# A two-layer transformer block on one core: first score maxima two tiles a block step, expert results two a step, closing projections in six pipelined steps

## The chip, the cores and the metric

The kernel runs on one core of one Trainium2 chip. The metric is the device time of one execution in microseconds, as the median of several runs. The engines are called as the profile calls them: PE (TensorE), DVE (VectorE), ACT (ScalarE), POOL (GpSimd) and SP (SyncE, which here only issues DMAs).

## The reference

Two transformer layers on x of B = 2 sequences, S = 1024 tokens and D = 128 channels, all float32:

```python
x = x + L0_attn(layernorm(x))   # 8 heads; q, k from low-rank latents, 128 + 32 wide; full softmax
x = x + L0_ffn(layernorm(x))    # shared FFN (width 352) + top-2 of 8 routed experts, per token
x = x + L1_attn(layernorm(x))   # 16 causal heads, 8 wide, with rotary embedding
x = x + L1_ffn(layernorm(x))    # 2 of 8 experts (GELU), chosen for a sequence by its first token
```

An FFN of layer 0 is `silu(x @ gate) * (x @ up) @ down`; a routed expert's result is weighted by its normalised router probability and added to the token's row. The second FFN is the mean of its two experts' results.

## The kernel before

**Stages.** Layer 0's attention runs to about 454 us. Its last pass carries the router of batch 0 beside it. Then comes the experts stage: the routed blocks of batch 0 (23 blocks of 128 tokens sorted by expert, plus two steps to drain), the shared expert for batch 0 and for batch 1 (two groups of 512 tokens each), and the routed blocks of batch 1. After it a short tail finishes the first score maxima of layer 1. Then eight passes `i = 1..8` do layer 1's attention, one group of four heads of one sequence each (`NG` = 4 groups): pass `i` finds the row maxima of group `i` beside the attention of group `i - 1`, so pass 8 has attention alone. Last come the closing projections and the second FFN of the last sequence.

**Order.** Most of the kernel is a set of Python generators. Each `yield` ends one step. A main generator is advanced by one step, then each of its "extras" by one; the engines' queues hold the instructions in just that program order, on PE, DVE, POOL and SP (and on ACT too up to pass 3), so nothing overtakes what stands ahead of it on its engine. `hurry(g, n)` runs n steps of g in one, `spread(g, n)` one step of g in n, `after(n, g)` starts g n steps later, and `wait_for(key, g)` holds g back until the key stands in the list `passed` (this is program order, not a wait on the chip). In the experts stage one main step is one routed block, or a third of a shared group's gate and up projection, or its down projection.

**What runs beside the experts stage.**
- `route(b)` (L287): layer norm, router logits, top two, then sums along tokens (`cums`, L321 and L324, on DVE) and their matmuls `rk` (L330 to L334), from which the sorted list of rows comes. Batch 0's is hurried by two beside layer 0's last pass, batch 1's by three in `rows1` (L965).
- The gathers of rows into blocks (L456, POOL), one a step where they run.
- `combine(b, half)` (L933): eight indirect DMAs on POOL (L938), each of which fetches 128 expert results of 64 KB from DRAM (`ys`, written by L919) and adds them to one column block of x, 4 column blocks for each of the two choices. For batch 0 they run beside the shared expert, one a step. The shared expert adds its own results to the same column blocks of x with a DVE add a group (L851).
- `heads0` (L1168 on): layer norm, Q and K of batch 0 for layer 1, each split in three bf16 parts (L1044 writes these to DRAM), and `fetch(0)`, then `fetch(1)` (L1078; 18 DMAs on SP each, L1085), which bring a group's parts back in the layout for the scores. `both_heads` starts each half when that half of `combine` has passed.
- `maxima(0)`: the first group's row maxima.

**The row maxima (`maxima(i)`, L1095).** A tile is 128 rows of four heads' scores: two matmuls (L1112), a mask (L1117) and a DVE reduction (L1122). A pass has 20 tiles in two halves. After each half the maxima are split in three bf16 parts (L1160, L1162 on POOL), transposed on PE (`tp_m`, L1126), and sent by DMA as three more rows of the scores' operands. The tiles' banks come from a PSUM pool of two slots, which the block steps' gate and up projections (`gub`, L880) and the shared expert's (`gu`, L834) share.

**After the experts stage** batch 1's results are combined (`results1`), then its heads (`heads1`), beside the tail and the first passes. `attend` (L1211) makes transposed scores (L1227), the exponential on ACT (L1232), the causal mask on POOL (L1236) and the values (L1252). `finish(b, half)` (L1331) closes half a sequence: for four strips of 128 tokens, transposes (L1339), reciprocal of the sums and product (L1344, L1346), and a transpose back (L1352, copied by ACT in L1353); then the output projection (L1357), its add to x (L1361), the layer norm, the first expert matmul (L1373), GELU (L1375), the second (L1381), the result (L1386) and its DMA (L1389).

Of the kernel before, what the change touches and what calls it, by code (L numbers as in the profile page):

```python
# [13 lines left out]
F32 = mybir.dt.float32  # L14
# [35 lines left out]
def two_layers(ctx: ExitStack, tc: tile.TileContext, a: dict, out: bass.AP):  # L50
# [128 lines left out]
    def spread(steps, n):  # L179

        for _ in steps:
            for _ in range(n):
                yield
# [30 lines left out]
    def after(n, steps, every=1):  # L214
        for _ in range(n):
            yield
        yield from spread(steps, every)
# [69 lines left out]
    def route(b, bank, spare):  # L287
# [34 lines left out]
        for i in range(3):  # L322
# [1 line left out]
            nc.vector.tensor_tensor(  # L324
                cums[i + 1][:, PAD:], cums[i][:, PAD:], cums[i][:, PAD - m : PAD + NT - m], ALU.add
            )
        yield
        yield
        rk = bank()[:, 0 : (NT + 1) * NE].rearrange("p (n e) -> p n e", e=NE)
        nc.tensor.matmul(rk[:, 0:NT], tri, h0[:, PAD:], start=True, stop=False)  # L330
        nc.tensor.matmul(
# [482 lines left out]
    def bank1():  # L814
        return sa.tile([P, 512], F32, tag="sa", name="bank1")
# [117 lines left out]
    def combine(b, half):  # L933

        pos = routed[b][1]
        for k in range(2):
            for n in range(4 * half, 4 * half + 4):
                nc.gpsimd.indirect_dma_start(  # L938
                    out=x[:, b * NT + n, :], out_offset=None, in_=ys_d[b],
                    in_offset=bass.IndirectOffsetOnAxis(ap=pos[:, k, n : n + 1], axis=0),  # L940
                    bounds_check=NBLK * P - 1, oob_is_err=True, compute_op=ALU.add,
                )
                yield
# [21 lines left out]
    def rows1():  # L965

        yield from hurry(route(1, bank1, spare1), 3)
        rows = get(1)
        while "blocks" not in passed:
            next(rows, None)  # L970
            yield
        for _ in range(2):
            next(rows, None)
            yield
        for half in range(2):
            for n, _ in enumerate(combine(0, half)):
                if n % 2:
                    next(rows, None)
                yield
            passed.append(half)  # L980
        yield from rows
# [91 lines left out]
    def wait_for(what, steps):  # L1073
        while what not in passed:
            yield
        yield from steps
# [18 lines left out]
    def maxima(i):  # L1095

        qp, kp = qkp[i % 3]
        mx = small.tile([P, 4, NT], F32, name="mx")
        mx2 = small.tile([P, 4, NT // 2, 2], F32, name="mx2")
        ready = []  # L1100

        def tile_of(st, c, heads):

            s0 = st * P
            c0, c1 = 512 * c, min(s0 + P, 512 * c + 512)
            w = c1 - c0
            sc = banks()
            if len(heads) == 4:
                sc = sc.rearrange("p a (b w) -> p (a b) w", b=2)
            for n, j in enumerate(heads):  # L1110
                diag = c1 == s0 + P
                nc.tensor.matmul(  # L1112
                    sc[:, n, 0:w], qp[0:KP, j, s0 : s0 + P], kp[0:KP, j, c0:c1],
                    start=True, stop=not diag,
                )
                if diag:
                    nc.tensor.matmul(  # L1117
                        sc[:, n, w - P : w], identb, mask_st, start=False, stop=True
                    )
            hs = slice(heads[0], heads[-1] + 1)  # L1120
            to = mx[:, hs, st] if st < NT // 2 else mx2[:, hs, st - NT // 2, c]
            nc.vector.tensor_reduce(to, sc[:, :, 0:w], AX.X, ALU.max, negate=True)  # L1122

        def send(half, mp):
            tp = sa.tile([48, P], BF16, tag="sa", name="tp_m")
            nc.tensor.transpose(tp, mp.rearrange("p k j n -> p (k j n)"), identb)  # L1126
            mt = small.tile([48, P], BF16, name="mt")
            nc.vector.tensor_copy(mt, tp)
            md = tc.dram_tile([48, P], BF16, name=f"md{i}_{half}")
            nc.sync.dma_start(md, mt)  # L1130
            nc.sync.dma_start(
                qp[KP : KP + 3, :, 512 * half : 512 * (half + 1)].rearrange(
                    "k j (n s) -> k j n s", s=P
                ),
                md.rearrange("(k j n) s -> k j n s", k=3, j=4),
            )

        def take():
            if ready and ready[0][0] == 0:
                ready.pop()[1]()  # L1140
            elif ready:
                ready[0][0] -= 1

        for half in halves(i):
            for st in range(4 * half + 3, 4 * half - 1, -1):
                for c in range(half + 1):
                    w = min(st * P + P - 512 * c, 512)
                    for heads in ((0, 1, 2, 3),) if w <= 256 else ((0, 1), (2, 3)):
                        tile_of(st, c, heads)
                        take()  # L1150
                        if (st, c, heads[-1]) != (4 * half, half, 3):
                            yield
            m4 = mx[:, :, 4 * half : 4 * half + 4]
            if half:
                nc.vector.tensor_tensor(m4, mx2[:, :, :, 0], mx2[:, :, :, 1], ALU.min)
            mp = small.tile([P, 3, 4, 4], BF16, name="mp")
            rest = m4
            for k in range(3):
                if k < 2:
                    nc.gpsimd.tensor_copy(mp[:, k], rest)  # L1160
                    r = small.tile([P, 4, 4], F32, name=f"mr{k}") if k == 0 else mp[:, 2]
                    nc.gpsimd.tensor_tensor(r, rest, mp[:, k], ALU.subtract)  # L1162
                    rest = r
            ready.append([1, lambda half=half, mp=mp: send(half, mp)])
            yield
        late.append(ready.pop()[1])

    def both_heads(b, xt):  # L1168

        halves = [heads(b, half, xt) for half in range(2)]  # L1170
        ready = [2 * b + half for half in range(2)]
        return [wait_for(n, after(6 if b == 0 else 3, h)) for n, h in zip(ready, halves)]

    def heads0():
        xt = xt_pool.tile([P, S], F32, name="xt")
        for _ in hurry(zip_longest(*both_heads(0, xt)), 2):
            yield
        yield
        passed.append("fetched")
        yield from after(4, fetch(1))  # L1180

    def results1():
        for half in range(2):
            yield from spread(combine(1, half), 2)
            passed.append(2 + half)

    def heads1():
        xt = xt_pool.tile([P, S], F32, name="xt")
        for _ in zip_longest(*both_heads(1, xt)):
            yield  # L1190

    late = []
    first_maxima = wait_for("fetched", maxima(0))
    with tc.manual_schedule(engines=ALL_IN_ORDER):
        for _, kp in qkp:

# [134 lines left out]
    def finish(b, half):  # L1331


        ot = o_pool.tile([P, 512], F32, name="ot")
        for i in range(4):
            s0 = (4 * half + i) * P
            tp = bank1().rearrange("p (h d) -> p h d", d=WH)
            for gr in range(NG):
                nc.tensor.transpose(  # L1339
                    tp[:, 4 * gr : 4 * gr + 4, :], us[NG * b + gr][:, s0 : s0 + P], ident  # L1340
                )
            yield
            rden = small.tile([P, H1], F32, name="rden")
            nc.vector.reciprocal(rden, tp[:, :, DH])  # L1344
            o = o_pool.tile([P, H1 * DH], F32, name="o")
            nc.vector.tensor_tensor(  # L1346
                o.rearrange("p (h d) -> p h d", d=DH), tp[:, :, 0:DH],
                rden.unsqueeze(2).to_broadcast([P, H1, DH]), ALU.mult,
            )
            yield  # L1350
            po = bank1()
            nc.tensor.transpose(po[:, 0:P], o, ident)  # L1352
            nc.scalar.copy(ot[:, i * P : (i + 1) * P], po[:, 0:P])  # L1353
            yield
        py = bank1().rearrange("p (n d) -> p n d", d=D)
        for i in range(4):
# [39 lines left out]
    for i in range(1, n + 1):  # L1396
        passes = []
        if i < n:
            passes.append(maxima(i))
        passes.append(attend(i - 1))  # L1400
        if i + 1 < n:
            extras.append(after(1, fetch(i + 1)))
        b, gr = divmod(i, NG)
        if gr == 1:
            extras.append(after(4, choose(b), 3))
        if gr == 0:

            first, other = halves(i - 1)
            extras.append(after(18 if first else 9, finish(b - 1, first)))
            extras.append(after(30, finish(b - 1, other)))  # L1410
        with tc.manual_schedule(engines=ALL_IN_ORDER if i < 4 else IN_ORDER):
            extras = beside(zip_longest(*passes), extras)
            if i == n:
                flush()
                extras = beside((), extras, True)
# [78 lines left out]
```

## Time and profile before

| what | value |
|---|---|
| median of 3 runs | 1015.2 us (1012.77 to 1024.3) |
| the profiled execution | 1025.0 us, span 1023.2 us, mean granted PE clock 0.927 |
| PE busy | 909.4 us (89% of the span) |
| DVE, ACT, POOL busy | 587.9, 424.2, 414.9 us |
| chain that ended last | PE 66%, DVE 17%, issue, DMA and POOL 4% each |

The page lists busy time of each engine, then its busy tenths in 40 slices of 25.6 us with the clock granted to PE, then the chain that ended last and the costliest groups of instructions. A row of the timeline reads: start and length in us, engine, line, operation, output and inputs, count, and in brackets the engine's idle time before it and what ended that. The waits view adds up such idle times: line and tile that waited, what for, us in total, how often, the longest. A busy PE includes matmuls at half clock.

### The profile page before, as it was taken

How to read it: one execution, taken by the hardware profiler on the slowest of the kernel's cores; microseconds unless marked ns; L12 is line 12 of the kernel's file. 1: busy time of each engine (PE TensorE's matmuls, PEld its weight loads, DVE VectorE, ACT ScalarE, POOL GpSimd, SP SyncE). 2: the span in 40 equal slices, each digit the busy share in tenths (PEclk: the TensorE clock that was granted, in tenths of full speed). 3: DMA queues.
4: the chain of work that ended last, by engine and by line, in shares of the span. 5: the costliest groups of instructions: out<-in, count | busy, mean ns of one | idle time of the engine just before them, and what ended most of it. 6: DMA issues, size and time to landing. Idle time of an engine off the chain costs nothing.

```text
span 1023.2 us, 14408 instructions
## 1 busy us (share of the span) xinstructions
PE 909.4 (89%) x5308; PEld 438.3 (43%) x5308; DVE 587.9 (57%) x1085; ACT 424.2 (41%) x694; POOL 414.9 (41%) x532
## 2 busy tenths in 40 slices
PE   3998999999999998999798996779889999899974
PEld 2533433333333333336675575433344445444333
DVE  4496454546564657746633573746755777467322
ACT  0102334444334344454231352224646765576741
POOL 2003727373846550265047510156672234144320
PEclk9799999999999999999899997859897998789987
DMA  9000000000000000014122233332312222120000
GB/s 277 15 1 1 1 2 1 1 1 1 1 2 1 1 1 21 6 34 92 26 60 29 39 69 84 70 49 35 83 36 59 33 36 32 35 40 13 3 0 21
DMA packets 34874, 33.49 MB, mean 33 GB/s; under 512 B 5804, under 2 KB 32332, under 8 KB 33644
## 3 DMA queue, kind: packets, MB, share of 16 engines
q1 hardware_dynamic: 24978, 24.09, 10.4%
q0 software_dynamic: 6592, 5.91, 4.1%
q10 hardware_dynamic: 3235, 2.58, 1.0%
q8 instruction: 43, 0.70, 0.3%
q14 instruction: 26, 0.21, 0.1%
HBM read 24.10 MB, written 8.45 MB: 32 GB/s over the span
## 4 chain that ended last, share of the span: by engine, by line
PE 66%; DVE 17%; issue 4%; DMA 4%; POOL 4%; ACT 4%; SPq 0%; POOLq 0%; ACTq 0%; DVEq 0%
PE sc L692 10%; PE sc L624 8%; PE up L1252 7%; PE ud L723 6%; PE banks L1112 5%; PE bank L1227 4%; DVE mx2a L628 4%; PE gub L880 4%; DVE rden L750 3%; DVE mx L1122 2%; PE sc L698 2%; PE gu L834 2%; PE yblk L908 2%; ACT ex L1232 1%; PE banks L1029 1%
## 5 line engine op out<-in xcount | busy, mean ns | idle before, releaser
L1122 DVE TENSOR_REDUCE mx<-banks 128x2 f32<-128x1024 f32 (+3 forms) x160 | 174.0, 1113 | 92.0 <-PE banks L1117 72.0
L628 DVE TENSOR_REDUCE mx2a<-sc 128x2 f32<-128x1024 f32 x128 | 153.8, 1219 | 113.3 <-PE sc L624 100.7
L703 ACT ACTIVATE ex<-sc 128x1024 f32<-128x1024 f32 x128 | 131.0, 1023 | 211.9 <-PE sc L698 208.8
L1232 ACT ACTIVATE ex<-bank 128x512 f32<-128x512 f32 (+2 forms) x320 | 155.9, 559 | 125.3 <-PE bank L1227 121.8
L711 POOL TENSOR_TENSOR sum<-sum,ex 128x1024 f32<-128x1024 f32 x60 | 140.1, 2349 | 38.0 <-ACT ex L703 38.0
L624 PE MATMUL sc<-key,q 64*128 64x512 f32 x512 | 149.4, 637 | 1.2 <-DVE mx2a L628 1.1
L692 PE MATMUL sc<-q,key 64*128 64x512 f32 x512 | 141.3, 616 | 8.6 <-DVE mx2a L628 8.4
L1112 PE MATMUL banks<-kp,qp 72*128 72x512 bf16 (+3 forms) x384 | 111.4, 362 | 18.3 <-DVE mx L1122 9.9
L1227 PE MATMUL bank<-qp,kp 75*128 75x512 bf16 (+3 forms) x384 | 100.5, 347 | 4.5 <-ACT ex L1232 2.8
L1236 POOL TENSOR_SCALAR_AFFINE_SELECT ex<-ex 128x128 f32<-128x128 f32 (+1 forms) x192 | 63.9, 368 | 89.3 <-ACT ex L1232 85.0
L456 POOL DMA_INDIRECT xb<-xn,row x46 | 53.0, 1152 | 103.0 <-DVE fblk L432 42.5
L1252 PE MATMUL up<-ex,vp 128*32 128x512 f32 (+3 forms) x768 | 85.6, 540 | 3.9 <-POOL ex L1236 3.9
L938 POOL DMA_INDIRECT x<-ys,pos x32 | 49.9, 1559 | 82.7 <-DMA kp<-parts 65.8
L692 PEld LDWEIGHTS sc<-q,key 64*128 64x128 f32 x512 | 49.6, 191 | 74.7 <-issue 43.1
L624 PEld LDWEIGHTS sc<-key,q 64*128 64x128 f32 x512 | 48.1, 190 | 73.5 <-issue 49.8
L723 PE MATMUL ud<-ex,val 128*32 128x512 f32 x512 | 69.5, 615 | 0.0
L1112 PEld LDWEIGHTS <-qp 72*128 72x128 bf16 x384 | 40.1, 107 | 66.2 <-issue 51.8
L880 PE MATMUL gub<-wall,xbt 128*128 x184 | 66.2, 486 | 1.8 <-ACT xbt L867 1.3
L708 POOL TENSOR_TENSOR sum<-ex,ex 128x1024 f32<-128x1024 f32 x12 | 28.2, 2347 | 74.2 <-ACT ex L703 74.2
L886 DVE TENSOR_TENSOR hds<-slb,gub 128x352 f32<-128x352 f32 x46 | 23.8, 517 | 57.0 <-ACT slb L885 56.8
L1117 PE MATMUL banks<-mask_st,identb 128*128 128x128 bf16 x256 | 53.5, 237 | 0.0
L698 PE MATMUL sc<-mr,onesb 64*128 64x512 bf16 x256 | 51.6, 382 | 0.0
(264 smaller groups left out, 1105.4 us busy)
## 6 DMA issues: line engine op xcount, KB each, us to landing
qp<-parts SPq DMA_DIRECT2D x72, 64.0 KB
kp<-parts SPq DMA_DIRECT2D x72, 64.0 KB
parts<-qk SPq DMA_DIRECT2D x24, 128.0 KB
ys<-yb SPq DMA_DIRECT2D x10, 256.0 KB
wall<-in_ffn_gate_dram SPq DMA_DIRECT2D x1, 1584.0 KB
wall<-in_ffn_up_dram SPq DMA_DIRECT2D x1, 1584.0 KB
wall<-in_ffn_down_dram SPq DMA_DIRECT2D x2, 576.0 KB
x<-in_h_dram SPq DMA_DIRECT2D x4, 256.0 KB
```

The costliest lines, as they stand in the source:

```text
L624: nc.tensor.matmul(sc[:, j, :], qs[i][pr][r, st * P : (st + 1) * P], key2[r, 512 * c : 512 * (c + 1)], start=True, stop=True,)
L628: nc.vector.tensor_reduce(mx2[:, 2 * pr : 2 * pr + 2, st, c], sc, AX.X, ALU.max, negate=True,)
L692: nc.tensor.matmul(sc[:, j, :], key2[r, k * P : (k + 1) * P], qs[i][pr][r, cols], start=True, stop=False,)
L703: nc.scalar.activation(ex, sc, AF.Exp)
L711: adder.tensor_tensor(sums[pr], sums[pr], ex, ALU.add)
L723: nc.tensor.matmul(ud[DC * j : DC * (j + 1), :], val[:, k, :], es[j // 2][:, j % 2, :], start=(k == 0), stop=(k == NT - 1),)
L880: nc.tensor.matmul(gu[:, s, 0:FF], xbts[j // 4][:, (j % 4) * P : (j % 4 + 1) * P], flat[:, bass.ds(e0 + FF * s, FF)], start=True, stop=True,)
L1112: nc.tensor.matmul(sc[:, n, 0:w], qp[0:KP, j, s0 : s0 + P], kp[0:KP, j, c0:c1], start=True, stop=not diag,)
L1122: nc.vector.tensor_reduce(to, sc[:, :, 0:w], AX.X, ALU.max, negate=True)
L1227: nc.tensor.matmul(sc[:, j, 0:w], kp[0 : KP + 3, j0 + j, t0 : t0 + P], qp[0 : KP + 3, j0 + j, lo:hi], start=True, stop=True,)
L1232: nc.scalar.activation(ex[:, :, 0:w], sc[:, :, 0:w], AF.Exp, scale=SCALE1)
L1252: nc.tensor.matmul(up[WH * j : WH * (j + 1), lo - c0 :], vps[b][:, k, h : h + WH], es[j], start=(k == 0), stop=end,)
```

## The change

It has five parts. (1) In `route`, two more steps lie between the running sums and their matmuls. (2) Batch 0's results are combined two a step beside the shared expert, with one gather behind each two; so its heads become free earlier in program order, and their start is set by 10 and 16 steps of waiting, where it was 6 for both; the wait between the last part written and `fetch(0)` grows from one step to three. (3) The first maxima run two tiles a step, and their bf16 parts are made on DVE. (4) Batch 1's results are combined one a step in place of one in two, and two fetches get guards. (5) `finish` works its four strips off in six steps, each of which holds the transposes of one strip, the products of the one before and the transposes back of the one before that; and in the last pass its second half starts after 21 steps in place of 30.

```diff
@@ -324,8 +324,8 @@
             nc.vector.tensor_tensor(
                 cums[i + 1][:, PAD:], cums[i][:, PAD:], cums[i][:, PAD - m : PAD + NT - m], ALU.add
             )
-        yield
-        yield
+        for _ in range(4):
+            yield
         rk = bank()[:, 0 : (NT + 1) * NE].rearrange("p (n e) -> p n e", e=NE)
         nc.tensor.matmul(rk[:, 0:NT], tri, h0[:, PAD:], start=True, stop=False)
         nc.tensor.matmul(
@@ -973,9 +973,8 @@
             next(rows, None)
             yield
         for half in range(2):
-            for n, _ in enumerate(combine(0, half)):
-                if n % 2:
-                    next(rows, None)
+            for _ in hurry(combine(0, half), 2):
+                next(rows, None)
                 yield
             passed.append(half)
         yield from rows
@@ -1155,11 +1154,12 @@
                 nc.vector.tensor_tensor(m4, mx2[:, :, :, 0], mx2[:, :, :, 1], ALU.min)
             mp = small.tile([P, 3, 4, 4], BF16, name="mp")
             rest = m4
+            eng = nc.gpsimd if i else nc.vector
             for k in range(3):
                 if k < 2:
-                    nc.gpsimd.tensor_copy(mp[:, k], rest)
+                    eng.tensor_copy(mp[:, k], rest)
                     r = small.tile([P, 4, 4], F32, name=f"mr{k}") if k == 0 else mp[:, 2]
-                    nc.gpsimd.tensor_tensor(r, rest, mp[:, k], ALU.subtract)
+                    eng.tensor_tensor(r, rest, mp[:, k], ALU.subtract)
                     rest = r
             ready.append([1, lambda half=half, mp=mp: send(half, mp)])
             yield
@@ -1169,28 +1169,30 @@
 
         halves = [heads(b, half, xt) for half in range(2)]
         ready = [2 * b + half for half in range(2)]
-        return [wait_for(n, after(6 if b == 0 else 3, h)) for n, h in zip(ready, halves)]
+        return [wait_for(n, after(wait, h)) for n, h, wait in zip(ready, halves, (3, 3) if b else (10, 16))]
 
     def heads0():
         xt = xt_pool.tile([P, S], F32, name="xt")
         for _ in hurry(zip_longest(*both_heads(0, xt)), 2):
             yield
-        yield
+        for _ in range(3):
+            yield
         passed.append("fetched")
         yield from after(4, fetch(1))
 
     def results1():
         for half in range(2):
-            yield from spread(combine(1, half), 2)
+            yield from combine(1, half)
             passed.append(2 + half)
 
     def heads1():
         xt = xt_pool.tile([P, S], F32, name="xt")
         for _ in zip_longest(*both_heads(1, xt)):
             yield
+        passed.append("heads1")
 
     late = []
-    first_maxima = wait_for("fetched", maxima(0))
+    first_maxima = wait_for("fetched", hurry(maxima(0), 2))
     with tc.manual_schedule(engines=ALL_IN_ORDER):
         for _, kp in qkp:
 
@@ -1332,25 +1334,30 @@
 
 
         ot = o_pool.tile([P, 512], F32, name="ot")
-        for i in range(4):
-            s0 = (4 * half + i) * P
-            tp = bank1().rearrange("p (h d) -> p h d", d=WH)
-            for gr in range(NG):
-                nc.tensor.transpose(
-                    tp[:, 4 * gr : 4 * gr + 4, :], us[NG * b + gr][:, s0 : s0 + P], ident
-                )
-            yield
-            rden = small.tile([P, H1], F32, name="rden")
-            nc.vector.reciprocal(rden, tp[:, :, DH])
-            o = o_pool.tile([P, H1 * DH], F32, name="o")
-            nc.vector.tensor_tensor(
-                o.rearrange("p (h d) -> p h d", d=DH), tp[:, :, 0:DH],
-                rden.unsqueeze(2).to_broadcast([P, H1, DH]), ALU.mult,
-            )
-            yield
-            po = bank1()
-            nc.tensor.transpose(po[:, 0:P], o, ident)
-            nc.scalar.copy(ot[:, i * P : (i + 1) * P], po[:, 0:P])
+        tps, os = {}, {}
+        for i in range(6):
+            if i < 4:
+                s0 = (4 * half + i) * P
+                tp = bank1().rearrange("p (h d) -> p h d", d=WH)
+                for gr in range(NG):
+                    nc.tensor.transpose(
+                        tp[:, 4 * gr : 4 * gr + 4, :], us[NG * b + gr][:, s0 : s0 + P], ident
+                    )
+                tps[i] = tp
+            if 0 <= i - 1 < 4:
+                tp = tps[i - 1]
+                rden = small.tile([P, H1], F32, name="rden")
+                nc.vector.reciprocal(rden, tp[:, :, DH])
+                o = o_pool.tile([P, H1 * DH], F32, name="o")
+                nc.vector.tensor_tensor(
+                    o.rearrange("p (h d) -> p h d", d=DH), tp[:, :, 0:DH],
+                    rden.unsqueeze(2).to_broadcast([P, H1, DH]), ALU.mult,
+                )
+                os[i - 1] = o
+            if i >= 2:
+                po = bank1()
+                nc.tensor.transpose(po[:, 0:P], os[i - 2], ident)
+                nc.scalar.copy(ot[:, (i - 2) * P : (i - 1) * P], po[:, 0:P])
             yield
         py = bank1().rearrange("p (n d) -> p n d", d=D)
         for i in range(4):
@@ -1399,7 +1406,7 @@
             passes.append(maxima(i))
         passes.append(attend(i - 1))
         if i + 1 < n:
-            extras.append(after(1, fetch(i + 1)))
+            extras.append(after(1, wait_for("heads1" if i + 1 == NG else "fetched", fetch(i + 1))))
         b, gr = divmod(i, NG)
         if gr == 1:
             extras.append(after(4, choose(b), 3))
@@ -1407,7 +1414,7 @@
 
             first, other = halves(i - 1)
             extras.append(after(18 if first else 9, finish(b - 1, first)))
-            extras.append(after(30, finish(b - 1, other)))
+            extras.append(after(30 if i < n else 21, finish(b - 1, other)))
         with tc.manual_schedule(engines=ALL_IN_ORDER if i < 4 else IN_ORDER):
             extras = beside(zip_longest(*passes), extras)
             if i == n:
```

## The prediction, made before the changed kernel was run

> **What bounds the kernel now.** I read the page from the top: engine shares, then the slices, then the waits and rows of the stretches that the change touches, and last the chain that ended last.
>
> ```profile
> PE 909.4 (89%) x5308; PEld 438.3 (43%) x5308; DVE 587.9 (57%) x1085; ACT 424.2 (41%) x694; POOL 414.9 (41%) x532
> ...
> PE   3998999999999998999798996779889999899974
> POOL 2003727373846550265047510156672234144320
> PEclk9799999999999999999899997859897998789987
> ```
>
> PE is the bound nearly everywhere. A change that leaves PE's work as it is, as this one does, can earn only where PE's digit is under 9: a slice is 25.6 us, so the dips to 8 and 7 at 384 and 486 us (the two route steps), to 6 7 7 from 614 to 691 us (fetch, first tiles, pass 1) and to 7 4 at the end. PEclk falls in or just behind them, so an idle PE is paid for a second time. The profiled execution took 1025.0 us (span 1023.2), the runs' median is 1015.2. I sum against 1025.0 and scale by 1015.2/1025.0 = 0.990.
>
> **1. Route: two more steps between the running sums and their matmul.** The rows of PE around the route's two ranks:
>
> ```profile
> 405.56 0.20 PE L330 MATMUL bank<-cum,tri 128*128 128x64 bf16 x1 [3.27 <-DVE cum L321]
> 406.23 0.21 PE L331 MATMUL bank<-cum,onesq 128*128 128x64 bf16 x1 [0.47 <-DVE cum L324]
> 406.38 2.08 PE L692 MATMUL sc<-q,key 64*128 64x512 f32 x4
> ...
> 493.14 0.20 PE L330 MATMUL bank<-cum,tri 128*128 128x64 bf16 x1 [3.27 <-DVE cum L321]
> ```
>
> In both, PE stands 3.27 + 0.47 = 3.7 us for a chain on DVE. Both routes are hurried (two and three of their steps in one main step), so two more yields put the matmul one main step later: 1.2 to 2.2 us of other matmuls go in front of it. I take 1.7 a route. The second gain is the clock: the four L692 after the stall took 2.08 us, four of them elsewhere in that stretch 1.13, and the block matmuls after the second stall 2.56 instead of 1.35. The Trainium skill ("TensorE: Matmul & The Clock Gate", "Part 1: The HAM clock gate") has the clock halved after an idle window of about 3.4 us and restored after as long a busy one; a stall shortened to 2 us falls under that, and the whole cold stretch goes: by that rule 1.7 us a route (half of 3.4, an estimate), by the rows 1.0 in the first four matmuls alone and as much again behind them. Twice (1.7 + 1.6) = **-6.5**, bounds -3 and -9. What is behind the matmul (list of rows, gathers) comes one step later; its gathers had several steps of slack in the trace.
>
> **2. Batch 0's results two a step: a new wait.** These accumulating DMAs add expert results into the tiles of x that the shared expert's add (L851) also writes.
>
> ```profile
> 543.80 0.69 DVE L851 TENSOR_TENSOR x<-bank,x 128x512 f32<-128x512 f32 x1 [2.59 <-PE bank L847]
> 552.85 0.69 DVE L851 TENSOR_TENSOR x<-bank,x 128x512 f32<-128x512 f32 x1 [2.59 <-PE bank L847]
> ```
> ```profile
> 544.76 1.54 POOL L938 DMA_INDIRECT x<-ys,pos  x1 [3.18 <-DVE x L851]
> 546.60 1.54 POOL L938 DMA_INDIRECT x<-ys,pos  x1 [0.30 <-issue]
> ...
> DMA to landing us min/median/max: 3.2/3.3/4.7
> ```
>
> Counted in program order, two DMAs are now ahead of the first L851, and all of half 1's are behind the second. They land just before 543.8, so they cost nothing. After the change four are ahead of the first, and twelve ahead of the second: half 1's first four included. POOL starts one each 1.85 us (544.76 to 546.60). Say the first still starts at 538.13. With the gather between them, the fourth starts at 545.04 and lands at 545.04 + 3.3 = 548.3, so the first L851 moves from 543.8 to 548.3. The fifth waits for that add (549.35), the twelfth starts seven later at 549.35 + 7 x 1.85 = 562.3 and lands at 565.6: the second L851 moves from 552.85 to 565.6. DVE is an in-order queue: behind the waiting add stand the silu products (L839, L840) of the next group, for which PE's down-projection waits, and the banks they free. PE would stand some 8.4 us, once its slots are full, and 2.6 at the first. The shift is 10.9 at the second group's end beyond what slack takes, plus about 2.1 of half clock afterwards: **+13**, bounds +3 (if PE gets further ahead than I think) and +15.
>
> Here a rule and the rows differ. The Trainium skill ("DMA: Bandwidth & Descriptors", "Anatomy of one DMA — SWDGE (gpsimd) path") fits 2.0 us + bytes/436e3, so 64 KB would land in 2.15 us (an estimate from that page); this trace has 3.3. By the rule the term is some 2 us less; I take the row. The same page's advice ("Rules for kernel authors"), issue early and wait late, speaks against this part: DMAs are put right ahead of an add that waits for them.
>
> **3. The first tile of batch 0.** Its Q and K arrive late:
>
> ```profile
> 631.83 1.01 PE L1112 MATMUL banks<-kp,qp 72*128 72x512 bf16 x2 [7.79 <-DMA ys<-yb]
> ...
> 633.27 2.55 PE L880 MATMUL gub<-wall,xbt 128*128 x4
> ```
>
> The releaser named is long done; the last load of fetch(0) (issued 625.4, L1085) is what lands at 631.6. The fetch moves three block steps earlier (a block step alone is 2.19 us), the tile one. Without part 2 the fetch lands at 631.6 - 6.6 and the tile is due at 624.0 - 2.2, a wait of 3.2 instead of 7.8. With part 2 both move 13: first tile at 638.2, so only +6.4 is left: **-6.6**. Bounds: -2.2 (the parts' way through DRAM isn't earlier) to -9.
>
> **4. Two tiles a step, parts on DVE.**
>
> ```profile
> PE tp_m L1126 <- POOL mp L1162: 10.1, 2, 5.6
> PE banks L1112 <- DMA ys<-yb: 7.8, 1, 7.8
> ```
>
> The 10.1 us: batch 0's parts queue on POOL behind batch 1's results (L938, 1.85 each). On DVE they are four small operations (POOL took 0.20 to 0.22 for three of them, 0.7 for the first), so about 1.0 in all stays exposed. Before, 8 steps with one tile took 2.74 each and 12 lone tiles 1.23 each (DVE's maxima, 1.1 each, set that). After, a step with two tiles: gate and up 1.19, transposes and down-projection 1.0, the second tile 0.44 after its bank comes free, the maxima 1.2: about 3.9, because both use the two slots of one PSUM pool. Nine of these, 2.5 of tail and 1.0 for parts: 638.2 + 38.6 = 676.8. Before, pass 1 began at 670.8. But the last block's ys now goes out about 20 us later in relation, and fetch(1)'s last load is issued at about 674; landing as fetch(0)'s did, pass 1 begins at 679: +8.2, of which 5.6 is given back since the second wait for POOL stood inside pass 1. So +2.6 where part 3 left +6.4: **-3.8**, bounds -8 and +3.
>
> **5. Batch 1's results one a round.** They need 16 x 1.85 = 29.6 us of POOL, and now start near 678 rather than 659, beside pass 1's selects (L1236), for which the values wait. A plain round takes 1.43 us, less than one DMA: POOL sets the first 14 rounds. I take +2.0 (bounds 0 and +6). Given back: batch 1's heads are through in pass 2, so its POOL work leaves the rounds where the values waited for POOL at 760 to 764 and PE ran on a half clock to 777; I take -2.8 of that 3.7 us wait and its cold stretch. Sum **-0.8**. The guards on the fetches never bind: what they wait for ends earlier in program order.
>
> ```profile
> core 0: us, PE busy (x) PEld busy (x) DVE busy (x) ACT busy (x) POOL busy (x), PEclk, DMA share, GB/s
> 652.00:671.00 19.00, 12.01 (x60) 6.43 (x59) 13.46 (x16) 0.00 (x0) 9.74 (x10) 0.58 0.43 73
> 671.00:721.40 50.40, 41.63 (x230) 17.55 (x229) 28.78 (x46) 20.64 (x42) 29.95 (x55) 0.79 0.29 40
> 984.00:1023.20 39.20, 20.13 (x84) 13.14 (x82) 11.58 (x38) 6.62 (x13) 4.12 (x12) 0.74 0.05 14
> ```
>
> **6. The end.** 39.2 us after the last attention, PE busy 20.1. The chain there, cut to the second half's part:
>
> ```profile
> 998.81 0.69 DVE res L1386
> ...
> 1003.59 1.72 PE bank L1357 x8
> 1005.33 0.70 DVE x L1361
> ...
> 1012.66 3.79 PE bank L1373 x4
> ```
>
> The second half's transposes, reciprocals and output projection come after the first half's FFN, one strip at a time (PE to DVE to PE to ACT, 1.5 us a strip). After the change the strips are pipelined and start nine rounds sooner, beside the first half's layer norm: the add of x (L1361) can follow the last attention by about 10.9 instead of 21 us. Then the two FFNs share PE, which is free for half of the stretch. -10 for this, +2 for what moves into attention where PE is full: **-8**, bounds -5 and -11. In passes 4 to 6 the same pipelining finds a busy PE: 0, bounds 1 either way.
>
> **Sum:** -6.5 + 13 - 6.6 - 3.8 - 0.8 - 8 = -12.7; 1012.3 of 1025.0, and times 0.990: **1003 us**.
>
> **Rivals.**
> - The add's wait is covered (PE works ahead while DVE stands; +2 in place of +13): 1001.3, scaled **992**. For it: PE's gate and up projections don't need L851. Against: two slots hold only one step.
> - The small gains fail: the route earns 2 (DVE was late by more than a step), the end 3 (its two FFNs collide on PE): -2 + 13 - 6.6 - 3.8 - 0.8 - 3 = -3.2, scaled **1012**. For it: chains of DVE and POOL, not PE, fill the end.
> - Slower: the clock stays low from the 8.4 us gap on through the double steps into pass 1. At half rate the L880 take 2.55 instead of 1.35, a double step about 2 us more: 9 x 2 = 18; pass 1 and 2's start at 0.58 instead of 0.79 would need 41.6 x 0.79/0.58 = 56.7 us of PE, 6 over the window. 1012.3 + 24 = 1036, scaled **1026**. For it: 0.58 was granted at 12.01 of 19.00 busy. Against: double steps are denser than that. It decides from a clock of 0.6 over those 90 us.
>
> **Chances.** Forecast 0.42 (own range 996 to 1010), covered add 0.18, small gains fail 0.20, cold clock 0.20. About 1% is what a measurement of this kernel can tell from no change. From the cases: faster 0.47, same 0.31, slower 0.22. The range takes in the covered case with the lower bounds of parts 1 and 6 (-7 from 992), and the cold case only to 1024.
>
> **What would show it.** Right: L330's waits about 2; L851 waiting for the DMA of L938, about 4.5 and 10 us; PE idle about 8 near 560; a first-tile wait near 3; no wait of tp_m for POOL in batch 0's tiles; about 29 us after the last attention instead of 39. Wrong if PE doesn't stand at the shared expert, if the end keeps its 39, or if the clock in the double steps is under 0.6.

## The result, and the profile after

The changed kernel took 1022.2 us (median of 20 runs, 1017.5 to 1026.4) against 1016.1 us for the kernel before (20 runs, 1010.1 to 1027.3): 1.006 of before, 95% interval 1.004 to 1.008. It is slower by 6 us; 1003 was forecast. On another chip the same pair gave 1.0046 (1.0026 to 1.0065).

The page of the changed kernel, the same rows as shown of before:

```profile
PE 899.8 (88%) x5308; PEld 431.8 (42%) x5308; DVE 589.7 (58%) x1093; ACT 425.2 (42%) x694; POOL 412.8 (40%) x524
...
PE   2998999999999998998895899867789999879985
POOL 2003727473837551075056330067454432315520
PEclk9699999999999999899999899959788999979998
```

Slices are 25.5 us. The end is better (8 5 in place of 7 4), and the slice from 613 us is a 9 where it was a 6. New are the 5 from 536 us, in the shared expert's stage, and 6 7 7 from 664 to 741 us, in passes 1 and 2, where before had 7 9 8. The low clock stays at 664 us (5).

I cut the traces at the same instructions (between passes to within 1.3 us). Each row is a stretch between them; "before, again" is the kernel with the route and end parts alone, or with the route part alone in passes 4 to 8 and the end. In the stretches quoted for it its instructions stand in before's order, so it is a second profile of before.

| stretch | before | before, again | after |
|---|---|---|---|
| second route's rank (L330) to the shared expert (L834) | 41.4 | - | 35.2 |
| shared expert, both batches | 38.0 | 37.9 | 53.8 |
| batch 1's blocks to the first tile | 59.3 | 59.6 | 50.0 |
| first tile to the end of batch 0's maxima | 39.0 | 38.3 | 34.3 |
| passes 1, 2, 3 | 50.6, 45.1, 35.6 | 49.6, 44.9, 31.0 | 58.4, 53.2, 29.0 |
| passes 4, 5, 6 | 29.5, 43.8, 50.9 | 29.5, 38.3, 48.8 | 29.5, 48.8, 46.3 |
| passes 7 and 8 | 57.4 | 59.5 | 60.5 |
| last values to the last result | 35.4 | 35.5 | 24.1 |

The two columns of before differ in passes 3 and 5 alone by more than 3 us: 35.6 against 31.0, and 43.8 against 38.3, with a clock of 0.84 against 0.98 and 0.88 against 1.00. The execution that the forecast was made from (1025.0 us, 9 over its median) had two stretches of half clock which an equal order of instructions doesn't always have. So I take the second column as the base from the first tile on. The first row holds a little more than a gain: 13 matmuls stand ahead of L330 in the changed kernel and behind it in before. L834 itself starts at 529.46 us in place of 534.54, so 5.1 us is gained up to there.

**The shared expert.** PE in the changed kernel's timeline, each row with the idle time before it:

```profile
544.73 1.96 PE L834 MATMUL gu<-xt,wall 128*96 128x512 f32 x4 [2.62 <-DVE hd L840]
...
562.01 3.73 PE L834 MATMUL gu<-xt,wall 128*96 128x512 f32 x4 [7.99 <-DVE hd L840]
```

The releaser named is the product behind which PE's bank comes free. That product stands on DVE behind L851, and these are the rows of L851 ahead of the two:

```profile
543.39 0.69 DVE L851 TENSOR_TENSOR x<-bank,x 128x512 f32<-128x512 f32 x1 [7.27 <-DMA x<-ys,pos]
...
560.67 0.69 DVE L851 TENSOR_TENSOR x<-bank,x 128x512 f32<-128x512 f32 x1 [12.64 <-DMA x<-ys,pos]
```

The second row of L834 runs at half clock as well: 3.73 us for what took 1.96 in the first.

**Pass 1.** PE's waits from 667.5 to 725.9 us (line, releaser: us in all, times, longest), and then what SP issued:

```profile
PE banks L1111 <- DMA kp<-parts: 6.7, 1, 6.7
PE tp_m L1125 <- POOL mp L1162: 4.8, 1, 4.8
PE up L1254 <- POOL ex L1238: 1.4, 2, 1.2
```
```profile
657.23 1.66 SPq L1084 DMA_DIRECT2D kp<-parts  x3
...
666.98 0.40 SPq L919 DMA_DIRECT2D ys<-yb  x1
667.44 1.04 SPq L1084 DMA_DIRECT2D qp<-parts  x3
668.52 0.97 SPq L1084 DMA_DIRECT2D kp<-parts  x3
```

The last block's results (L919) are ready only at 667, and the last six loads of fetch(1) stand behind them in SP's queue. They land at 674.7, PE waits 6.7 us, and the pass starts on a low clock. The wait did not bring the clock down, though. It began at 668, and the last tiles of the tail run at half clock from 666.0 on: the same matmul took 0.27 us at 665.82 and 0.42 at 666.26.

```profile
665.82 0.27 PE L1111 MATMUL banks<-kp,qp 72*128 72x256 bf16 x1 [0.64 <-DVE mx L1121]
...
666.26 0.42 PE L1111 MATMUL banks<-kp,qp 72*128 72x256 bf16 x1
...
674.70 1.01 PE L1111 MATMUL banks<-kp,qp 72*128 72x512 bf16 x2 [6.74 <-DMA kp<-parts]
```

Then POOL: batch 1's results and pass 1's selects take turns, and the bf16 parts of pass 1 stand behind both.

```profile
696.39 1.69 POOL L938 DMA_INDIRECT x<-ys,pos  x1 [0.17 <-issue]
697.57 1.07 POOL L1238 TENSOR_SCALAR_AFFINE_SELECT ex<-ex 128x128 f32<-128x128 f32 x2
698.81 1.57 POOL L938 DMA_INDIRECT x<-ys,pos  x1 [0.17 <-issue]
```

A round is 2.4 us here (696.39 to 698.81); a plain one takes 1.43.

### The profile page after: what moved, and what is told of

Same layout as the page of the kernel before. It is cut to its first block, busy times and chain, and to the rows that moved or that the text cites. A ratio compares the mean times of both kernels' runs of the same rounds, so it can differ in the third digit from the quotient of the medians.

```text
span 1021.4 us, 14424 instructions
## 1 busy us (share of the span) xinstructions
PE 899.8 (88%) x5308; PEld 431.8 (42%) x5308; DVE 589.7 (58%) x1093; ACT 425.2 (42%) x694; POOL 412.8 (40%) x524
## 5 line engine op out<-in xcount | busy, mean ns | idle before, releaser
L692 PE MATMUL sc<-q,key 64*128 64x512 f32 x512 | 142.2, 620 | 8.6 <-DVE mx2a L628 8.4
L1111 PE MATMUL banks<-kp,qp 72*128 72x512 bf16 (+3 forms) x384 | 105.1, 347 | 18.8 <-DVE mx L1121 11.4
L456 POOL DMA_INDIRECT xb<-xn,row x46 | 52.3, 1137 | 109.8 <-DVE fblk L432 45.9
L692 PEld LDWEIGHTS sc<-q,key 64*128 64x128 f32 x512 | 49.2, 190 | 75.8 <-issue 42.6
L624 PEld LDWEIGHTS sc<-key,q 64*128 64x128 f32 x512 | 48.0, 190 | 73.5 <-issue 49.8
L1116 PE MATMUL banks<-mask_st,identb 128*128 128x128 bf16 x256 | 51.5, 229 | 0.0
```

The costliest lines, as they stand in the source:

```text
L624: nc.tensor.matmul(sc[:, j, :], qs[i][pr][r, st * P : (st + 1) * P], key2[r, 512 * c : 512 * (c + 1)], start=True, stop=True,)
L692: nc.tensor.matmul(sc[:, j, :], key2[r, k * P : (k + 1) * P], qs[i][pr][r, cols], start=True, stop=False,)
L1111: nc.tensor.matmul(sc[:, n, 0:w], qp[0:KP, j, s0 : s0 + P], kp[0:KP, j, c0:c1], start=True, stop=not diag,)
```

## The experiments

All ratios are to the kernel before, on the same chip and in the same series. They were run in four series, on four chips; before took 1024.9, 1026.7, 1024.1 and 1013.9 us there.

**The kernel before once more.** No edit.

> The kernel before, profiled once more. The profiled execution of before took 1025.0 us, 9 over the median of its runs (1016.1). If that excess is spread clock noise, this profile shows the same waits and total near 1016; if it is one place (a cold stretch behind one wait), one stage of this profile is 5 us or more shorter than in the first and the others agree within 1 us.

One execution took 1039.1 us, against a median of 1024.9 on that chip. It settled part of the question: passes 3 and 5 were again long (35.7 and 40.7), but 11.5 us more lay in the stretch before the shared expert, where PE waited 5.9 us for a releaser that the profile doesn't show. One execution of before can thus be 14 us over its median, and at more than one place.

**Batch 0's results behind the adds.**

```diff
-        for _ in range(2):
+        for _ in range(4):
             next(rows, None)
             yield
         for half in range(2):
             for _ in hurry(combine(0, half), 2):
...
-... zip(ready, halves, (3, 3) if b else (10, 16))]
+... zip(ready, halves, (3, 3) if b else (6, 12))]
```

> The changed kernel with batch 0's results two steps later, so that each DMA stands behind the shared expert's add to the same part of x, and the waits of the heads shortened by as much: order on PE, DVE, ACT and SP unchanged. Theory (the adds' wait for the accumulating DMAs costs the shared stage 15.8 us): L851 waits for no DMA, PE's 8.0 and 2.6 us before L834 go, the stage is 38 to 40 us instead of 53.8; some of it comes back as a wait of the first tile for its fetch (3 to 7 us), so 8 to 11 us in all: about 1012, 0.996 of before. Rival (the stage is slack, since the heads' chain of DMAs sets the first tile anyway): the first tile starts where it did, time 1020 to 1022, 1.004 to 1.006.

0.9934 (0.9911 to 0.9957): 11 to 13 us better than the changed kernel's own two ratios. The shared stage is 41.4 us, and L851 waits for no DMA any more, only for its own matmul:

```profile
  PE bank L847: 10.3, 4
```

The first tile's wait did not come back (49.8 us from the blocks to it), so more was kept than I expected. The order of PE, DVE, ACT and SP is that of the changed kernel, and on POOL one gather stands two places earlier. What makes the 12 us is which of the two writers of x is first in program order, and so which waits: POOL now stands 20.7 us until L851 is through, and PE waits for neither.

**fetch(1) two steps earlier.**

```diff
-        yield from after(4, fetch(1))
+        yield from after(2, fetch(1))
```

> The changed kernel with fetch(1) two steps earlier, so that its last six DMAs stand ahead of the last block's ys write in SP's queue and not behind it. Theory (that write holds SP until 667.0, and pass 1 waits 6.7 us for the loads behind it and then runs on a low clock): the 6.7 us wait goes, pass 1's clock rises from 0.69 to 0.79 or more: -8 to -11 us, about 1013. Rival (pass 1 is set by POOL, which has 16 results and the selects in its queue): pass 1 starts 7 us earlier and ends within 2 us of where it did, about 1020.

1.0015 (0.9994 to 1.0036): 3 to 5 us better than the change, well short of the 8 to 11 that I expected. Pass 1 went from 58.4 to 51.8 us, its clock only from 0.69 to 0.73, and pass 2 got 1 us longer. The wait was there and went; the low clock did not begin with it. In this run too the clock fell to half ahead of the pass, at 672.6 us, where its first tile starts at 676.0 without a wait for a DMA.

**The pipelined end alone**, on the kernel before (the hunk of `finish` and the start at 21 steps).

> The kernel before with the six pipelined steps of the end and the second half's start at 21 steps alone. Theory (the end gains 11 us after the last values, the attention ahead of it loses 3): -8 us, 0.992 of before. Rival (what moves into attention, or the halves closed in passes 4 to 6, costs as much as it brings): 0.998 to 1.002.

0.9973 (0.9959 to 0.9988): -2.8 us, between the theory and the rival. The end itself gained what was forecast (35.4 to 23.6 us). Pass 5 gave back most of it. Its windows without the new end (route part alone) and with it (start and end, length, then PE busy; PEclk is the third from the end):

```profile
834.50:872.80 38.30, 36.02 (x279) 18.44 (x277) 29.48 (x55) 22.64 (x49) 12.67 (x44) 1.00 0.22 34
```
```profile
840.30:888.10 47.80, 41.82 (x307) 22.83 (x306) 32.34 (x67) 28.97 (x55) 13.04 (x43) 0.96 0.20 33
```

The shorter `finish` brings part of its FFN from pass 6 into pass 5 (PE 279 to 307 matmul records; pass 6 goes from 48.8 to 45.9), which is only a move. But PE's idle time in pass 5 goes from 2.3 to 6.0 us: strips that follow each other closely make PE wait for DVE's products (L1350) and for the GELU, which were spread out before. The size of the loss depends on the base: passes 5 and 6 together took 87.1 (the one above) to 95.1 us in six profiles without the new end, 91.6 in the mean, and 92.6 to 96.4 in ten with it, 94.8 in the mean. The medians' -2.8 us is the better measure.

**The changed kernel again**, no edit.

> The changed kernel again, on this chip beside before. If its 0.6% loss belongs to the program, the ratio is 1.004 to 1.008 again and the profile shows the shared stage at 53.8 us and pass 1's 6.7 us wait; if chips differ in how they take it, the ratio moves by more than 0.4%.

1.0046 (1.0026 to 1.0065), with a shared stage of 52.3 us and a wait of 6.2 us for fetch(1): the loss belongs to the program.

**Both repairs.** The two diffs together.

> The changed kernel with both repairs: batch 0's results behind the shared adds, and fetch(1) two steps earlier. Theory (the two losses are in different stages and add: some 13 us and some 4.6 us): 0.988 to 0.991 of before. Rival (POOL sets pass 1: with an earlier start it only waits longer there): 0.992 to 0.995, no better than the first repair alone (0.9934).

0.9895 (0.9861 to 0.9928): they add.

**The route's two steps alone**, on the kernel before (the first hunk).

> The kernel before with the route's two more steps alone. Theory (the stall of 3.7 us in layer 0's last pass only moves, since the clock drops after 2.0 us too, and the one in the experts stage gives 3.5 us and up to 2 more of half clock): -3 to -5 us, 0.995 to 0.997. Rival (the gain is taken back behind it, where the gathers for the next blocks come one step later): 0.999 to 1.001.

0.9887 (0.9834 to 0.9941): -6 to -17 us, more than I expected. Taken from the pair with the end (0.990 below, less 0.9973) it is -7.5 us. The traces agree that it can be worth more than in the first pair: in the first of the four series the stretch from L330 to L834 took 51.5 and 52.9 us in the two profiles without the edit, and 42.8 and 43.1 in the two with it.

**Batch 0's results two a step alone**, on the kernel before; the heads' waits are lengthened to 14 and 22 so that they stand where they stood.

> The kernel before with batch 0's results two a step alone, the heads held back by as many steps more so that they stand where they stood. Theory (the adds wait for DMAs): shared stage 51 to 54 us in place of 38, of which the first tile's wait for its fetch (7.8 us) takes up little, since the fetch moves with it: +11 to +14 us, 1.011 to 1.014. Rival (the stage's loss is taken up by slack before the first tile): 1.000 to 1.004.

1.0107 (1.0044 to 1.0169): +11 us. The shared stage took 49.5 us in place of 38.0, and the first tile came as long after it as before (59.4 against 59.3): nothing took it up.

**The tiles' part alone**, on the kernel before: tiles two a step, parts on DVE, heads and fetch(0) at the changed places, the guards on the fetches; batch 1's results stay at one in two rounds.

> The kernel before with the third part alone: first maxima two tiles a step, their parts on DVE, heads and fetch(0) as early as in the change, fetch(1)'s last six loads behind the last ys write as there; batch 0's results one a step and batch 1's one in two, as before. Theory (the tiles' stage gains some 13 us, and what is lost in passes 1 and 2 comes from batch 1's results, which no longer lie beside the lone tiles but beside pass 1, so it is lost here too): passes 1 to 3 take 135 us or more in place of 126, sum within 3 us of before, 0.997 to 1.003. Rival (the loss is the one-a-round pace of batch 1's results, which is not in here): passes 1 to 3 at 126 to 130 plus the 6.7 us wait for the fetch, 0.990 to 0.995.

1.0258 (1.0226 to 1.029): +26 us, and both expectations were wrong. The blocks and tiles gained 9 us, then the loads of two groups came late:

```profile
682.57 1.01 PE L1112 MATMUL banks<-kp,qp 72*128 72x512 bf16 x2 [6.87 <-DMA kp<-parts]
...
824.23 1.01 PE L1112 MATMUL banks<-kp,qp 72*128 72x512 bf16 x2 [11.85 <-DMA kp<-parts]
```

The first is fetch(1). The second is the first group of batch 1, whose heads now come too late. With two tiles a step the tail has hardly a step left, so what advances by one step a round comes as many rounds later. In before, 6 of batch 1's 16 results start ahead of pass 1, the last at 718.5 us, and the heads' first matmul (L1029) at 710.7. Here it is 3 results, 748.7 and 740.8, though pass 1 starts only 12 us later. That is what the results one a round are there for.

**Both repairs, batch 1's results one in two rounds.**

```diff
-            yield from combine(1, half)
+            yield from spread(combine(1, half), 2)
```

> The changed kernel with both repairs and batch 1's results one in two rounds again. Theory (place, not pace: POOL has the same DMAs in front of pass 1's selects, only further apart, and batch 1's heads come later): within 0.4% of the kernel with both repairs (0.9895), 0.987 to 0.993. Rival (the pace makes POOL the bound of pass 1, rounds of 2.3 to 2.7 us between 688 and 705): 0.982 to 0.986.

1.0013 (0.9991 to 1.0034), 12 us worse than one a round, so both expectations fell. Pass 1 is down to 40.1 us from 55.4 in the kernel with both repairs, but the same late group costs 12.1 us at the end of pass 3. The pace in the change is forced, and it costs pass 1.

**Both repairs, pass 1's parts on DVE too.**

```diff
-            eng = nc.gpsimd if i else nc.vector
+            eng = nc.gpsimd if i > 1 else nc.vector
```

> The changed kernel with both repairs and pass 1's bf16 parts on DVE too. Theory (the 4.8 us wait of the transposes for POOL in pass 1 and the half clock of some 12 us behind it go): -6 to -9 us against both repairs, 0.981 to 0.984 of before. Rival (PE then waits for the selects, which stand behind the same DMAs): 0.987 to 0.990.

0.9896 (0.9866 to 0.9927), no gain on both repairs: the rival. Pass 1 took 55.6 us against 55.4 with the parts on POOL; the 4.8 us wait went, and PE's wait for POOL's selects went from 2.2 to 4.5 us, so the wait mostly moved.

**Route and end alone**, on the kernel before.

> The kernel before with the two parts that helped alone: the route's two more steps (0.9887 by itself) and the pipelined end (0.9973 by itself). If the parts add: 0.984 to 0.988. If part of the route's gain was chance: 0.990 to 0.993.

0.990 (0.9874 to 0.9925), where the parts alone would give 0.986, so part of the 0.9887 may be chance. It is the same as the whole change with both repairs, so the repaired tiles' part (tiles two a step, parts on DVE, results one a round, heads earlier) is worth nothing within 0.4%.

**The first group's parts on DVE alone**, on the kernel before (the hunk with `eng`, nothing else).

> The kernel before with batch 0's bf16 parts made on DVE alone, everything else as before. Theory (the two waits of the transposes for POOL, 4.5 and 5.6 us, and the half clock behind them are worth their 10 us by themselves, and the change loses them to the moved results of batch 1): -7 to -12 us, 0.988 to 0.993. Rival (in the parts' place POOL's results and pass 1's selects set the pace, so the waits only move): 0.997 to 1.001.

0.9892 (0.9864 to 0.992): -11 us. The windows of the first tiles, pass 1, 2 and 3, first of route and end alone (parts on POOL), then of this kernel:

```profile
634.10:672.40 38.30, 30.06 (x165) 20.32 (x166) 26.33 (x34) 6.62 (x13) 9.59 (x10) 0.77 0.29 53
672.40:722.00 49.60, 40.85 (x222) 16.87 (x222) 28.78 (x45) 20.68 (x41) 29.56 (x53) 0.79 0.26 39
722.00:766.90 44.90, 38.55 (x246) 16.16 (x244) 29.05 (x56) 25.32 (x52) 30.19 (x58) 0.90 0.28 67
766.90:797.90 31.00, 30.30 (x244) 14.95 (x243) 21.79 (x23) 22.15 (x45) 12.43 (x36) 0.98 0.26 50
```
```profile
634.50:668.60 34.10, 30.20 (x165) 20.45 (x166) 26.94 (x38) 6.63 (x13) 6.20 (x4) 0.80 0.30 56
668.60:712.90 44.30, 41.11 (x229) 17.33 (x229) 29.41 (x50) 20.63 (x41) 31.64 (x52) 0.83 0.34 48
712.90:758.00 45.10, 38.74 (x244) 16.42 (x243) 29.18 (x57) 25.34 (x52) 30.52 (x58) 0.89 0.30 66
758.00:788.60 30.60, 29.89 (x244) 14.69 (x243) 21.59 (x23) 22.16 (x45) 11.84 (x36) 0.99 0.27 50
```

The two waits of the transposes for POOL are gone from the first two windows (4.2 and 5.3 us shorter), and nothing comes back in the other two. The changed kernel has this edit, and its same four windows are 34.3, 58.4, 53.2 and 29.0 us: 174.9 in all against 154.1, so what the edit earns was spent, and more. Most of it went in pass 1: 44.3 us here with batch 1's results one in two rounds, 55.4 in the kernel with both repairs, where they come one a round (and the heads with them).

**Route, end and the parts of passes 0 and 1 on DVE**, on the kernel before.

> The kernel before with the route's steps, the pipelined end, and the bf16 parts of passes 0 and 1 on DVE. If the parts' gain adds to 0.990: 0.978 to 0.983, the fastest here. If it is absorbed in pass 1: 0.988 to 0.991.

0.9832 (0.979 to 0.9873): 995.5 us against 1013.9 on its chip, the fastest here, at the edge of what adding up gives. It beats both kernels, with tiles, results and heads where they were before.

## Why the prediction was wrong

The sum was -12.7 us of a profiled execution; measured in the same stretches it is +10 (the medians moved by +6, and the difference is within what single executions differ by).

| part | forecast | measured |
|---|---|---|
| 1 route | -6.5 | -5.1 up to the shared expert; alone -7.5 to -11.6 |
| 2 batch 0's results | +13 | +15.8 in the stage; alone +11, undone -11 to -13 |
| 3 first tile | -6.6 | -9.3 |
| 4 and 5, tiles to pass 3 | -4.6 | 163.8 to 174.9: +11.1 |
| 6 end | -8 | -2.4 in passes 4 to 8 and the end; alone -2.8 |

- **Part 1** came near in size, but not in place, so that is luck: half was to come from each route. PE's rows of the two ranks after the change:

```profile
406.43 0.20 PE L330 MATMUL bank<-cum,tri 128*128 128x64 bf16 x1 [1.99 <-DVE cum L321]
...
407.25 2.08 PE L692 MATMUL sc<-q,key 64*128 64x512 f32 x4
...
494.23 0.19 PE L330 MATMUL bank<-cum,tri 128*128 128x64 bf16 x1
```

  The first route's wait only fell from 3.27 to 1.99 us, and the four L692 behind it took the same 2.08 us: nothing was won there. The second gave all of it: its matmul no longer waits, and the cold stretch behind it is gone.
- **Part 2** held step by step. Counted from the stage's start the two adds moved by 4.7 and 12.9 us where 4.5 and 12.75 were forecast, and PE's waits were 2.6 and 8.0 us where 2.6 and 8.4 were. The DMAs took the 3.3 us of the row to land again, and not the 2.15 us estimated from the Trainium skill ("DMA: Bandwidth & Descriptors", "Anatomy of one DMA — SWDGE (gpsimd) path"). The rival in which PE works ahead fell with it.
- **Part 3** was low: no wait was left at the first tile, where I had left 3.2.
- **Parts 4 and 5 are the step that failed**, by 16 of the 23 us between -12.7 and +10. The double steps did better than forecast (the tiles ended at 667.7, and the fetch landed at 674.7 where I had 679). Wrong was what I let come back, "5.6 is given back since the second wait for POOL stood inside pass 1", and the +2.0 for POOL in pass 1. Batch 0's wait did go, but pass 1's own parts took its place behind batch 1's results (4.8 us, idle and then half clock). I had priced the 16 DMAs by POOL's time alone, and their pace is what cost: pass 1 took 44.3 us with one in two rounds (the first group's parts alone), 55.4 with one a round (both repairs), and 40.1 when the repaired kernel went back to one in two, which moves the heads back too. The slower pace was not to be had either: the lone rounds of the tail were gone, and batch 1's first group then came 12.1 us late. Passes 1 and 2 took 111.6 us in place of 94.5:

```profile
667.50:725.90 58.40, 44.86 (x222) 18.05 (x220) 29.36 (x54) 20.20 (x40) 36.42 (x54) 0.69 0.33 50
725.90:779.10 53.20, 43.65 (x264) 20.12 (x262) 32.13 (x52) 28.10 (x56) 33.40 (x58) 0.84 0.26 61
```

  Against the rows of route and end alone (above), 8.0 of the 17.1 us is idle time of PE, which now includes 6.7 for the fetch behind the ys write; 9.1 is busy time, at a lower clock and with 18 matmul records more.
- **Part 6**: the end itself gained 11.3 us, as forecast; "in passes 4 to 6 the same pipelining finds a busy PE: 0" was wrong. Passes 4 to 8 together lost 9 us against the route part alone, 10.5 in pass 5 alone, with 2.5 back in pass 6; that base was the fastest of six profiles in passes 5 and 6.
- **The base**: I took the waits of one execution that stood 9 us over its median as if all of them were in every one. The scale of 0.990 spread that excess evenly; it sat in passes 3 and 5.

The slower rival named a low clock from the shared expert into pass 1. Its place was half right (pass 1 at 0.69), its mechanism not: the double steps ran at 0.98, and the clock fell at 666.0, in the last lone tiles. The rival of small gains came near in the end's size (3, where 2.4 to 2.8 was measured) by another cause: what was lost was lost in passes 4 to 8, and not where its two FFNs meet.

Left open: how the remaining loss of passes 1 and 2 (some 10 us with both repairs) divides between POOL's turns and batch 1's heads. No run moved one without the other in the repaired order.

## What to carry to other kernels

Before a slow stretch is shortened, list what runs beside it and what is paced by its rounds: a tail in which PE idles is cover, and with fewer rounds all that takes one step a round comes later, or must be hurried into passes that are full. Of an accumulating DMA and an engine's add to the same tile, let the one wait that holds up nothing else, and a write that is ready late must not stand ahead of loads in one queue. Here a change in five parts was slower than before although three of its edits, one of them a little widened, are worth 1.7% (18 us) without the rest, so try the parts one by one.

## What the runs showed of the hardware

- An idle PE of 1.99 and 0.47 us on end halved its clock in the first route (L692: 2.08 us, where 1.13 is usual), while one of 2.62 us in the shared expert did not (L834: 1.96 us, where half clock shows 3.73). The length alone didn't decide; the 3.4 us of the Trainium skill ("TensorE: Matmul & The Clock Gate", "Part 1: The HAM clock gate") would have spared both, and the measurement decides. In both kernels' profiles the changes of the clock lie whole multiples of 3.41 us apart (405.8, 409.2, 436.5 and 439.9 us in before), and where a stall falls in these steps fits better: in the step up to 406.6 us PE was busy for 1.41 us, while the 2.62 us are split over two steps (539.7 to 546.6) with 2.41 and 1.83 us busy. No threshold comes out of it: 2.10 us busy in the step up to 666.0 were followed by half clock.
- In the last blocks of batch 0, PE stood for 3 to 6 us with no releaser in the profile, in before and in changed kernels alike (5.9 us in the kernel before once more), but not in the two profiles that the forecast and the result rest on, nor in the two of the last series. I can't name the cause; it makes that stretch unfit for comparing single profiles.
